# Reordering a four-layer network on one core: layer 0's attention as one chain, layer 2's attention behind the gathers row by row

## The chip, the cores and the metric

The kernel runs on one core of one Trainium2 chip. A core has a matrix engine (TensorE, "PE"; its weight loads are listed apart as "PEld"), a vector engine (VectorE, "DVE"), a scalar engine for activations (ScalarE, "ACT"), a general engine (GpSimd, "POOL") that also issues the indirect DMAs here, and a sync engine (SyncE, "SP") that issues most of the other DMAs. Each engine works through its own list of instructions in order and waits on semaphores of the others. The metric is the device time of one execution in microseconds. A profile is one execution taken by the hardware profiler; its span covers the first to the last recorded instruction.

## The reference

The input x has 4 rows of 1024 tokens with 128 features, in f32. Four layers follow, each an attention (or a recurrence) and a feed-forward, each added to x and normalised:

```
x = layernorm(x + L0_attn(x));  x = layernorm(x + L0_ffn(x))
x = layernorm(x + L1_attn(x));  x = layernorm(x + L1_ffn(x))
x = layernorm(x + L2_attn(x));  x = layernorm(x + L2_ffn(x))
x = layernorm(x + L3_attn(x));  x = layernorm(x + L3_ffn(x))
```

- L0_attn: a projection, a causal convolution over 4 tokens, and cumulative sums along the tokens: with v a projected value and p_w a positive weight, the sums of p_w·poly(v)·cos(theta·v), p_w·poly(v)·sin(theta·v) and p_w for 4 values of theta. The ratio, normalised by its mean square, goes through small matrices, a gate and an output projection.
- L0_ffn: x and the weight are rounded to a 6-bit float grid in blocks of 32 with a scale each, then one linear map.
- L1_attn: a diagonal complex recurrence, h[t] = a·h[t-1] + B·x[t], y = C·Re(h).
- L1_ffn: a mixture of 16 experts (4 chosen per token, within 2 of 4 groups) and a shared one; each is silu(x·gate)·(x·up)·down.
- L2_attn: causal softmax attention with 16 heads of 8 and rotary positions.
- L2_ffn: a mixture of 8 experts, 2 chosen, that share common matrices, each with a low-rank correction of rank 16.
- L3_attn: a gated mixing along the tokens with Toeplitz matrices. L3_ffn: 32 experts, 4 chosen, and a shared one.

A token's result in L0_attn and L1_attn depends on the earlier tokens of its row; in L2_attn it depends on all earlier tokens of the same row, in L3_attn on all tokens of its row. Rows are independent of each other, and the feed-forwards work token by token.

## The kernel before

**Tiles and parts.** x stays in SBUF as 32 tiles of 128 tokens. A "quarter" q is 256 tokens of each of the 4 rows, 8 tiles; quarters 0 and 1 are called the first half (part a), 2 and 3 the second half (part r in layer 1). Tile `q*8 + b*2 + k` holds the k-th 128 tokens of quarter q of row b.

**Mixtures of experts.** `l1_route` computes each token's experts and the place of each (token, expert) pair in a list sorted by expert. `spread` (L1305 on) then issues one indirect DMA per tile and chosen expert on POOL, 64 for a half in layer 1, each writing 128 rows of x to the list in HBM. `l1_experts` reads the list in blocks of 4 tiles (`xg`), transposes them, multiplies them with the weights of the block's expert (in a "wall" of all experts' weights in SBUF, 3 MB for layer 1) and writes the results to another list. `l1_close` gathers them back (`collect`, L1359: 64 indirect reads on POOL into buffers `yt`, four to a buffer, five buffers), adds them to x with the routing weights, normalises, saves x to HBM and makes the transposed xT that the next layer reads. `zero_lists` clears the lists first.

**The order of the work.** Each stage is a Python generator that emits instructions and yields a cost. `run` goes through one generator alone. `mix(main, side, pace, drain)` goes through `main` and, after each of its yields, takes from `side` until the yields' costs balance; what `side` emits is put on each engine's list behind the latest instruction of `main`. `chain` puts generators one behind the other, `abreast` lets several advance together by cost, `when` holds a generator back until a name is in `self.listed`, and `press` (L1824) draws from a side generator until a condition holds. A framework then orders each engine's list and puts in semaphores. The order of all stages is written out in `all()`:

1. `l0_attn` of quarters 0 and 1 alone. Its multiplications by `pq` go to POOL; with `no_pool` they go to DVE. `prepare(q+1)` is emitted within quarter q. For each of 4 thetas: t, k (the rounding of t, by adding and taking away a large number RND), sin and cos on ACT, a multiplication by pq, a scan on DVE (`l0_scan`), a square on ACT, matmuls.
2. `l1_setup`, `l2_setup`, then `l0_ffn` of quarters 0 and 1 alone (its `quantize` passes between DVE and POOL), then `l1_attn` of quarters 0 and 1 mixed with `l2_weights`. The latter builds the 24 weight tiles of layer 2's 8 experts: a small matrix `am` on POOL, matmuls, a copy on ACT, a write to HBM.
3. `l1_route(a)`. Then `l0_attn` of quarters 2 and 3 (no_pool) mixed with `spread` of part a.
4. `l1_wall` (weights), `l1_experts(a)` mixed with `l0_ffn` and `l1_attn` of quarters 2 and 3; `l1_shared(a)` and what is left of that, mixed with `l1_close(a)` quarter by quarter.
5. `l1_wall` again, `l2_attn(0)`, that is the first half's attention, mixed with `l1_route(r)` and `spread` of part r.
6. `l2_wall`, `l1_experts(r)` and `l1_shared(r)` mixed with layer 2's routing and spread of part a2; `l2_experts(a2)` mixed with `l1_close(r)`.
7. `l2_attn(1)` and all later stages.

`norm(tiles, by)` takes mean and variance on DVE, the reciprocal root on ACT, POOL or DVE by the argument `by`, and applies both with one DVE instruction a tile (L205).

## Time and profile before

| | us |
|---|---|
| median of 15 runs | 2542.91 |
| lowest, highest | 2538.28, 2558.33 |
| profiled execution, its own time | 2538.07 |
| its span | 2536.3 |

| stage (profiled execution) | about, us from the span's start |
|---|---|
| layer 0 attention, quarters 0 and 1 | 0 to 130 |
| layer 0 feed-forward, quarters 0 and 1 | 145 to 205 |
| layer 1 attention, quarters 0 and 1, with layer 2's weight tiles | 205 to 285 |
| layer 1 routing of part a | 285 to 312 |
| layer 0 attention, quarters 2 and 3, beside the spread of part a | 312 to 426 |
| layer 1 experts of part a | 434 to 540 |
| shared experts, rest of quarters 2 and 3 | 540 to 602 |
| gathers of part a | 541 to 648 |
| layer 2 attention, first half (first scores at 667.6) | to 928 |
| spread of part r, inside it | 726 to 807 |

How the profile is read: "busy" is the time in which an engine worked on instructions of a group or a stretch. A line of a group gives the source line, engine, operation, the tiles written and read, the count, the total and the mean duration of one, and behind the bar the idle time of the engine just before them and what ended it. A line of a stretch gives start and end, length, busy time and number of instructions for PE, PEld, DVE, ACT and POOL, the granted TensorE clock, the share of the DMA engines and GB/s. The chain of work is followed back from the last instruction: at each step to what released it, or to the instruction before it on its engine. "Another core or an unknown queue" and "remote" in it mean a wait whose end the profile cannot put down to a recorded instruction.

### The profile page before, as it was taken

Reading aid. Unit: us, or ns where it says so; the run is one execution under the profiler, and the core shown is the slowest. Engines: PE = TensorE matmul, PEld = TensorE weight load, DVE = VectorE, ACT = ScalarE, POOL = GpSimd, SP = SyncE. Lnnn points to the kernel's source line nnn. Section 1 sums busy time; section 2 is a strip of 40 time slices with the busy share of each in tenths; the row PEclk is TensorE's granted clock in tenths of the full one; section 3 lists DMA queues with packets and bytes.
Section 4 is the critical chain, followed back from the end, with each engine's and each line's share of the span. In section 5 each row is a group of like instructions: output and inputs, shape, how many; then the busy total and the mean of one; then the engine's idle time right before and its main releaser. Section 6 shows DMA issues by size and latency. Waiting matters only on the chain.

```text
span 2536.3 us, 28615 instructions
## 1 busy us (share of the span) xinstructions
PE 1698.1 (67%) x9605; PEld 1030.5 (41%) x9605; DVE 1350.1 (53%) x3797; ACT 810.8 (32%) x1158; POOL 779.7 (31%) x725
## 2 busy tenths in 40 slices
PE   7538676863652875797797888758619896754810
PEld 3225333752220454555432332336316683642710
DVE  8864796856560662344556663735403565631453
ACT  5512362320320432222375545512102352310310
POOL 5432185235145004233310001020560203154364
PEclk9768787986775997898898988979859997876965
DMA  9902002331001143222300000030410331321421
GB/s 318 289 16 83 19 35 105 104 129 42 21 28 40 53 147 107 73 62 61 110 20 1 1 6 12 14 128 22 176 57 18 106 105 44 92 85 53 117 77 53
DMA packets 224007, 192.05 MB, mean 76 GB/s; under 512 B 16816, under 2 KB 204080, under 8 KB 222832
## 3 DMA queue, kind: packets, MB, share of 16 engines
q1 hardware_dynamic: 203152, 147.28, 18.5%
q0 software_dynamic: 20704, 42.86, 5.1%
q8 instruction: 83, 1.36, 0.2%
q14 instruction: 68, 0.56, 0.1%
HBM read 93.47 MB, written 96.60 MB: 75 GB/s over the span
## 4 chain that ended last, share of the span: by engine, by line
PE 43%; DVE 22%; another core or an unknown queue 13%; POOL 9%; issue 8%; ACT 3%; DMA 3%; SPq 0%; DVEq 0%; POOLq 0%; ACTq 0%
PE gu L157 11%; PE s L157 10%; PE yp L157 5%; PE tp L165 5%; PE sc L157 5%; POOL l1ra L1293 4%; POOL yt L1293 2%; PE pu L157 2%; PE pg L157 1%; DVE x L1359 1%; PE py L157 1%; DVE pr L1055 1%; ACT pr L1049 1%; DVE x L205 1%
## 5 line engine op out<-in xcount | busy, mean ns | idle before, releaser
L1049 ACT ACTIVATE pr<-sc 128x1024 f32<-128x1024 f32 x288 | 279.5, 1021 | 319.2 <-PE sc L157 191.0
L157 PE MATMUL gu<-ld,xgT 128*128 x768 | 203.7, 408 | 47.4 <-DVE hg L1689 15.6
L157 PE MATMUL sc<-qm,kT 32*128 32x512 f32 (+3 forms) x1536 | 201.3, 559 | 15.6 <-ACT pr L1049 11.7
L157 PE MATMUL s<-pr,va 128*32 128x512 f32 (+3 forms) x1536 | 176.9, 526 | 48.2 <-issue 28.1
L157 PE MATMUL gu<-wall,xgT 128*128 x352 | 180.7, 640 | 20.1 <-DMA wall<-wall 18.0
L165 PE MATMUL tp<-ld,hg 128*128 128x128 f32 x736 | 118.8, 284 | 95.4 <-DVE hT L169 52.5
L157 PEld LDWEIGHTS gu<-ld,xgT 128*128 128x128 f32 x768 | 145.7, 201 | 79.4 <-issue 23.7
L169 DVE COPY hT<-tp 128x512 f32<-128x512 f32 x140 | 96.0, 686 | 138.5 <-remote 72.3
L165 PEld LDWEIGHTS tp<-ld,hg 128*128 128x128 f32 x736 | 94.5, 147 | 153.2 <-issue 58.9
L1055 DVE TENSOR_TENSOR pr<-pr,ld 128x512 f32<-128x512 f32 (+1 forms) x160 | 92.4, 580 | 102.2 <-ACT pr L1049 95.9
L1689 DVE TENSOR_TENSOR hg<-sg,gu 128x256 f32<-128x256 f32 x192 | 78.5, 417 | 123.6 <-ACT sg L1688 109.1
L1462 ACT ACTIVATE sg<-gu 128x512 f32<-128x512 f32 x88 | 52.5, 598 | 276.4 <-PE gu L157 166.8
L157 PEld LDWEIGHTS sc<-qm,kT 32*128 32x128 f32 x1536 | 86.3, 198 | 120.1 <-issue 73.7
L167 ACT COPY xgT<-tp 128x512 f32<-128x512 f32 x118 | 69.2, 586 | 182.0 <-PE tp L165 129.3
L1688 ACT ACTIVATE sg<-gu 128x256 f32<-128x256 f32 x192 | 72.9, 385 | 162.7 <-PE gu L157 105.0
L165 PE MATMUL tp<-ld,xg 128*128 128x128 f32 x472 | 78.9, 292 | 64.2 <-DMA xg<-l3rb 15.0
L1464 DVE TENSOR_TENSOR hg<-sg,gu 128x512 f32<-128x512 f32 x88 | 60.1, 683 | 112.4 <-ACT sg L1462 93.3
L1293 POOL DMA_INDIRECT l1ra<-x,posl1a x64 | 94.3, 1474 | 60.7 <-DVE posl1a L1270 41.5
L1293 POOL DMA_INDIRECT yt<-l1yr,posl1r x64 | 60.5, 945 | 151.4 <-DVE x L1359 82.0
L157 PE MATMUL yp<-ld,hT 128*128 x768 | 104.2, 278 | 4.3 <-issue 3.5
L157 PEld LDWEIGHTS s<-pr,va 128*32 128x32 f32 x1536 | 38.2, 111 | 157.9 <-issue 110.5
L157 PE MATMUL yp<-wall,hT 128*128 x704 | 99.9, 289 | 1.5 <-DVE hT L169 1.5
(433 smaller groups left out, 3529.5 us busy)
## 6 DMA issues: line engine op xcount, KB each, us to landing
wall<-wall SPq DMA_DIRECT2D x16, 768.0 KB
l3ra<-zero SPq DMA_DIRECT2D x1, 6144.0 KB
wall<-we SPq DMA_DIRECT2D x24, 256.0 KB
ld<-in_l_w SPq DMA_DIRECT2D x2, 3072.0 KB
ld<-in_l_w SPq DMA_DIRECT2D x1, 6144.0 KB
xg<-l3ra SPq DMA_DIRECT2D x24, 256.0 KB
l3ya<-yg SPq DMA_DIRECT2D x24, 256.0 KB
l1ra<-zero SPq DMA_DIRECT2D x1, 5120.0 KB
```

The lines of the kernel that those rows point to most:

```text
L157: return self.nc.tensor.matmul(out, lhsT, rhs, start=start, stop=stop)
L165: nc.tensor.transpose(pt[:, k * P : (k + 1) * P], s, self.ident)
L167: nc.scalar.copy(dst, pt[:, : n * P])
L169: nc.vector.tensor_copy(dst, pt[:, : n * P])
L205: nc.vector.tensor_scalar(x, x, mv[:, t, 0:1], rstd[:, t : t + 1], ALU.subtract, ALU.mult)
L1049: nc.scalar.activation(pr, sc[h], AF.Exp)
L1055: nc.vector.tensor_tensor(d, d, cst["tril"].unsqueeze(1).unsqueeze(1).to_broadcast([P, 2, n, P]), ALU.mult)
L1293: ins = self.nc.gpsimd.indirect_dma_start(**kw)
L1462: nc.scalar.activation(sg, gu[:, 0, :], AF.Silu)
L1464: nc.vector.tensor_tensor(h, sg, gu[:, 1, :], ALU.mult)
L1688: nc.scalar.activation(sg, pg[:, :, 0, :], AF.Silu)
L1689: nc.vector.tensor_tensor(h[:, 2 * c : 2 * c + 2, :], sg, pg[:, :, 1, :], ALU.mult)
```

## The change

- `l0_attn` takes all four quarters as one main generator; only quarter 3 has `no_pool`. Its side, at pace 0.8, is, in this order: layer 1's and layer 2's setup and the clearing of lists (`after(0)`), `l0_ffn` and `l1_attn` of quarter 0, the same of quarter 1, `l1_route` of part a1, and `spread` of a1 abreast of `l2_weights`. Part a1 is the first half with its tiles in the order of rows.
- `l1_shared(a1)` comes ahead of `l1_experts(a1)`; both are mixed with `l0_ffn` and `l1_attn` of quarters 2 and 3.
- `l1_close` goes by rows instead of quarters: 16 gathers, the additions, the norm of 4 tiles, the transposes, and the name "row" is listed. It now lies, with `l1_route(r)` and the spread of r, beside `l2_attn(0)`, whose `prepare(b)` presses the side until row b is listed.
- `l1_wall` for part r is loaded after `l2_attn(0)`, together with `l2_wall`.
- The first addition of the rounding (k) moves from DVE to ACT; the cosine is written over k; t, sq and den, and pools of `l0_ffn` and `l1_attn`, have fewer buffers.
- In layer 0 and in layer 1's attention the norm is applied on ACT (`on_act`), with a small extra DVE instruction; `am` moves from POOL to ACT; one multiplication of `l1_attn` in the first half moves from POOL to DVE.

```diff
+    def norm(self, tiles, by="act", on_act=False):
...
+        if on_act:
+            off = self.tile(self.small, [P, n], f"off{n}")
+            nc.vector.scalar_tensor_tensor(off, mv[:, :, 0], -1.0, rstd, ALU.mult, ALU.mult)
         for t, x in enumerate(tiles):
-            nc.vector.tensor_scalar(x, x, mv[:, t, 0:1], rstd[:, t : t + 1], ALU.subtract, ALU.mult)
+            if on_act:
+                nc.scalar.activation(x, x, AF.Identity, bias=off[:, t : t + 1], scale=rstd[:, t : t + 1])
+            else:
+                nc.vector.tensor_scalar(x, x, mv[:, t, 0:1], rstd[:, t : t + 1], ALU.subtract, ALU.mult)
...
-                    t = self.tile(tp, [P, QC], "t")
-                    nc.scalar.activation(t, xv, AF.Copy, scale=self.turn[:, m : m + 1])
+                    turn = self.turn[:, m : m + 1]
+                    t = self.tile(tp, [P, QC], "t", bufs=1)
+                    nc.scalar.activation(t, xv, AF.Copy, scale=turn)
                     k = self.tile(tp, [P, QC], "k")
-                    ts(k, t, RND, None, ALU.add)
+                    nc.scalar.activation(k, xv, AF.Identity, scale=turn, bias=self.rnd)
...
-                    re = self.tile(tp, [P, QC], "re")
+                    re = k
...
-                        times(v, v, pq, ALU.mult)
+                        times(q)(v, v, pq, ALU.mult)
...
+        nc, x, hf = self.nc, self.x, part.q0 // 2
+        xTv = self.xT.rearrange("p (q b t) -> p b q t", q=NQT, b=B)
+        for b in range(B):
+            yield from self.collect("l1", part, K1, yp, b * 4, 4)
+            tiles = part.order[b * 4 : b * 4 + 4]
+            self.norm([x[:, t, :] for t in tiles], by="dve")
+            for t in tiles[::2]:
+                nc.sync.dma_start(out=self.xsave[:, t : t + 2, :], in_=x[:, t : t + 2, :])
+            yield (5.0,)
...
+            nc.vector.tensor_copy(xTv[:, b, 2 * hf : 2 * hf + 2, :], pt.rearrange("p (q t) -> p q t", q=2))
+            self.listed.add(f"row {hf}{b}")
...
             def prepare(b):
+                self.press(side, lambda: f"row {hf}{b}" in self.listed)
...
-                    nc.gpsimd.tensor_scalar(am, ab[:, i, :], self.cst["em"][:, e : e + 1], 2.0, ALU.mult, ALU.mult)
+                    nc.scalar.activation(am, ab[:, i, :], AF.Copy, scale=em[:, e : e + 1])
...
+    def after(self, q):
+        yield from self.when(lambda: f"l0 {q}" in self.listed)
+        if q == 0:
+            self.l1_setup()
+            yield (20.0,)
+            self.l2_setup()
+            self.zero_lists("l1")
+            yield (4.0,)
...
-                self.run(self.l0_attn((0, 1)))
-                self.l1_setup()
-                self.l2_setup()
-                weights = self.l2_weights()
-                next(weights)
-                self.zero_lists("l1")
-                self.run(self.l0_ffn((0, 1)))
-                self.run(self.mix(self.l1_attn((0, 1)), weights))
-                self.run(self.l1_route(a))
-                self.run(self.mix(self.l0_attn((2, 3), True), self.spread("l1", a, K1)))
+                main = self.l0_attn(range(NQT), (NQT - 1,))
+                side = self.chain(
+                    *(g for q in range(2) for g in (self.after(q), self.l0_ffn((q,)), self.l1_attn((q,)))),
+                    self.l1_route(a1), self.abreast(self.spread("l1", a1, K1), self.l2_weights()),
+                )
+                self.run(self.mix(main, side, pace=0.8))
...
-                    side = self.chain(self.l0_ffn((2, 3), True), self.l1_attn((2, 3), True))
-                    self.run(self.mix(self.l1_experts(a, wall), side, drain=False))
-                    self.run(self.mix(self.chain(self.l1_shared(a), side), self.l1_close(a, yp)))
+                    side = self.chain(*(g for q in (2, 3) for g in (self.l0_ffn((q,)), self.l1_attn((q,)))))
+                    self.run(self.mix(self.chain(self.l1_shared(a1), self.l1_experts(a1, wall)), side))
+            with ExitStack() as c2:
+                yp = self.pool(c2, "l1ya", 5, right=True)
+                side = self.chain(self.l1_close(a1, yp), self.l1_route(r), self.spread("l1", r, K1))
+                self.run(self.mix(self.l2_attn(0, side), side))
             with ExitStack() as c2:
                 wall = self.l1_wall(c2)
-                self.run(self.mix(self.l2_attn(0), self.chain(self.l1_route(r), self.spread("l1", r, K1))))
                 wall2 = self.l2_wall(c2)
```

## The prediction

> **What bounds the kernel now.** I read the page first. No engine is full: TensorE is busy 67% of the span, and 13% of the chain that ended last is put down to nothing that the profile knows.
>
> ```profile
> PE 1698.1 (67%) x9605; PEld 1030.5 (41%) x9605; DVE 1350.1 (53%) x3797; ACT 810.8 (32%) x1158; POOL 779.7 (31%) x725
> PE 43%; DVE 22%; another core or an unknown queue 13%; POOL 9%; issue 8%; ACT 3%; DMA 3%; SPq 0%; DVEq 0%; POOLq 0%; ACTq 0%
> ```
>
> The built programs have the same order on every engine from the second layer 2 attention on (about 1250 us), so only the time before that can change. I cut it into stages; each line gives the stretch, its length and busy time per engine.
>
> ```profile
> 20.00:78.00 58.00, 45.52 (x171) 19.25 (x170) 52.47 (x42) 39.13 (x45) 34.75 (x12) 0.89 1.05 307
> 78.00:130.00 52.00, 29.80 (x129) 13.39 (x128) 42.06 (x53) 25.74 (x33) 19.78 (x8) 0.72 1.03 289
> 130.00:205.00 75.00, 25.75 (x123) 17.32 (x121) 46.92 (x123) 8.53 (x16) 22.92 (x15) 0.68 0.01 2
> 205.00:285.00 80.00, 66.48 (x269) 41.07 (x268) 36.14 (x90) 17.89 (x32) 16.51 (x23) 0.87 0.22 79
> 285.00:312.00 27.00, 21.14 (x68) 9.62 (x72) 22.69 (x124) 14.72 (x15) 0.00 (x0) 0.82 0.00 1
> 312.00:414.00 102.00, 74.24 (x332) 33.04 (x322) 94.00 (x120) 59.40 (x67) 85.47 (x55) 0.85 0.09 35
> ...
> 434.00:540.00 106.00, 92.57 (x580) 79.13 (x579) 84.27 (x212) 38.37 (x79) 18.96 (x8) 0.97 0.32 95
> 540.00:602.00 62.00, 35.00 (x140) 22.82 (x140) 30.41 (x76) 5.85 (x10) 34.41 (x32) 0.75 0.30 104
> 602.00:668.00 66.00, 17.77 (x57) 8.61 (x60) 37.59 (x154) 8.17 (x12) 31.70 (x33) 0.56 0.16 49
> 735.00:815.00 80.00, 16.61 (x68) 5.48 (x68) 7.54 (x33) 2.05 (x2) 54.98 (x58) 0.54 0.12 48
> ```
>
> The third number after a stretch's length is VectorE. It is slack in 130 to 285 (layer 0's feed-forward and layer 1's attention of the first half) and full in 312 to 414 (layer 0's attention of the second half beside the spread). In 735 to 815 nothing works but GpSimd, which issues the spread of the second half's rows, in the middle of layer 2's attention. The chain and the waits show that stall, and a smaller one at 554:
>
> ```profile
> 554.42 14.65 another core or an unknown queue
> ```
> ```profile
> 732.60 12.33 another core or an unknown queue
> 747.47 21.29 another core or an unknown queue
> 769.81 46.67 another core or an unknown queue
> ```
> ```profile
> ACT pr L1049 <- remote: 79.2, 2, 66.9
> ```
>
> The two spreads differ in one thing: VectorE was busy 0.92 beside the first, 0.09 beside the second.
>
> ```profile
> L1293 POOL DMA_INDIRECT l1ra<-x,posl1a x64 | 94.3, 1474 | 60.7 <-DVE posl1a L1270 41.5 <-issue 19.2
> L1293 POOL DMA_INDIRECT l1rr<-x,posl1r x64 | 61.8, 965 | 97.8 <-DVE posl1r L1270 78.6 <-issue 19.2
> ```
>
> With the 0.30 us of issue the slow one has a pitch of about 1.78, the fast one 1.27 us. Pairing each TensorE result in the trace with its first reader: the reader starts 0.06 us (mean of 1311) after TensorE's last record if GpSimd issued no indirect DMA in the 15 us before, 0.88 after 1 to 8, 2.13 after 9 to 11, and 7.47 (40 cases) after 12 or more. What makes that lag the trace does not say. I call it the crawl and use it as a price: a full-pitch burst nearly stops work that passes from TensorE to another engine.
>
> **Part by part**, against the profiled execution's 2538.07 us (median of the runs 2542.91, 4.8 above; I add the difference to the median).
>
> 1. Layer 0's attention in one chain, first half's next layers behind it. The first quarter has nothing beside it and ends at about 78, as before. VectorE's instructions up to the end of layer 1's routing, taken in the changed order at before's mean durations, are 282 us, 56 of them by 78. Cross-check: 316 to the experts' start before, less 16 rounding adds of 0.777 (now on ScalarE), 19 of normalisations (ScalarE too), 9 multiplies of 1.215 (third quarter, now GpSimd), plus about 4 for the additions, is 277 with a 4 us tail behind routing: 273. ScalarE gains this work and has room: the same count gives it 184. At 0.92, the row of 312 to 414, the remaining 226 take 246: routing ends at 324 (before 312). Ends: 304 at a full VectorE, 354 at the 0.81 of 78 to 130.
>
> 2. The spread begins there, but only a 4 us tail of layer 0's attention is left for VectorE, so it runs at 1.27: 81 us, to 405 (before 426). What stood beside the old spread stood 102 us; now little is beside it. GpSimd's queue holds layer 0's feed-forward of the third quarter behind the spread.
>
> 3. Layer 2's weight tiles moved from beside layer 1's attention (where they cost nothing visible) to beside the spread. On TensorE's queue all 24, then the shared experts and that feed-forward, stand ahead of the experts. A tile passes TensorE to ScalarE with two PSUM buffers: at the crawl (7.5 + 0.6 copy + 1.2 back) / 2 = 4.65 us, so from 331 (half of the layer 1 wall's 9 us of DMA behind routing) 16 are done at 405; 8 at 1.83 (44 us of TensorE in 24) end at 420. Then shared experts 23 (38 before less the 14.65 stall) and 6 for the feed-forward's interleaved matmuls (its GpSimd chain, 16 us from 444 to 460 before, runs 409 to 425 alongside). Experts start at 450, before 434: +16. Ends: 415 without any crawl; 493 if TensorE makes 0.6 records per us, half of the old stall's 104 in 81 us: the 72 tile and 8 attention matmuls then end at 464, plus 29. On SP the experts' wall waits behind twelve of the tiles' writes and for layer 0's last matmuls, so it is late with them, not besides.
>
> 4. Experts and the rest of the side. By the count of part 1 VectorE has 111 us to do between the end of layer 0's attention and that of layer 1's attention of the fourth quarter, some 16 of them before the experts; the 95 left, the 0.795 of 434 to 540, are 119: 569, before 602. The gain so far is 33.
>
> 5. Closing by rows. Two rows' 32 gathers, between 1.25 and the 1.67 of this stage: 45, then 20 from the last gather to the first scores as before (648 to 667.6): 634, before 667.6. **Gain 33.** The title's "first row" is two in VectorE's order: rows 0 and 1 both stand ahead of the attention's main work.
>
> 6. The other two rows' gathers now lie inside layer 2's attention. Twenty may run ahead (five buffers of four) and come at full pitch: 25 us at 75 lost of 81 is 23. The other twelve 3. VectorE gets 22 us of adds and norms there, of which its idle 0.27 takes most: 7. **+33**; ends 0 (gathers thinned out, below 9 in 15 us) and 50. ScalarE and TensorE queue behind VectorE's block of 44 instructions.
>
>    The Trainium skill ("SBUF — State Buffer", "A bandwidth-pool intuition that's wrong") says that a DMA with descriptors made by GpSimd took about 620 ns alone and 3100 beside VectorE's copies. Here the row beside a VectorE at 0.92 is 1474 against 965 ns. No row comes near 3100. By the page's figure 32 gathers would be 99 us instead of 45, an estimate, and the sum some 50 us higher.
>
> 7. The second spread moves from 35% to 82% of layer 2's attention, with 128 TensorE instructions left; the old stall let 104 through in 81 us. So it costs the same there, plus its last landing now open (431 less 426 before): **+4**. Ends -10 and +25.
>
> 8. Layer 1's wall, 3 MB, was loaded at 541 under other work; now it waits for the end of layer 2's first attention, behind five expert loads on SP and ahead of layer 2's wall. Its first load took from 420 to about 430: **+10**. Ends 0 (under the spread) and 20.
>
> 9. Normalisation on ScalarE elsewhere, 16 saves for 4, ScalarE instead of GpSimd for small scalings: off the path while the spreads and VectorE bound; nothing. Without that cover, 16 issues on SP at the 0.3 of a GpSimd issue are 5 us.
>
> Sum: -33 + 33 + 4 + 10 = **+14**. 2543 + 14 = **2557 us**.
>
> **Rivals.**
> - *Faster (0.32).* The weight tiles and rows do not crawl. With parts 1 and 3 at 415, experts and side end at 534, first scores at 599 (-69); of part 6 the 7 remain, the rest as above: -69 + 21 = -48; halfway -20. For it: the lag was seen mostly with attention's two passes per tile, and the old first spread had none. Against: that spread was slow. It decides from experts earlier than 436.
> - *Much slower (0.17).* The exposed spread crawls at 0.6 records per us, experts at 493: +57. For it: the 735 to 815 line. Against: copies to ScalarE need one pass only.
> - *Wash (0.09).* As my case, but the gathers inside the attention take 20 instead of 33: +1.
> - *Not what it says (0.08).* If the attention in effect waits for all four rows, gathers of 107 us as before from 569 give scores at 696: the gain of 33 becomes 28 lost, but part 6 vanishes: +42.
>
> **Numbers.** My case, +5 to +35 (2548 to 2578), has 0.34, little more than the faster one, from which the crawl alone parts it; I take it because the row nearest to the new first spread is the second of before, at full pitch with VectorE idle. With the two slower rivals, slower has 0.59. A measurement of this kernel tells about 0.2%, 5 us, from no change: within it lies the wash, 0.09; faster has 0.32. The range leaves a tenth out at each end: below, the faster case's better third (from -40, 2503, to -48 and past it); above, what goes beyond the much slower case's +57 with a few microseconds of parts 7 and 8 (2607).
>
> **What would show it.** Right: first spread's indirects near 0.97 us and VectorE idle beside it, weight tiles unfinished at its end, experts around 450, first scores around 634, a stall of about 80 us late in the first layer 2 attention, then a 10 us hole before the experts of the second half. Wrong: routing after 350 (VectorE starved by one-buffer tiles of layer 0), experts before 436, scores before 610, or a difference that arises after 1250.

## The result

The changed kernel takes 2657.78 us (median of 9 runs, 2645.94 to 2665.94); before took 2543.2 (47 runs). The ratio is 1.0444, 95% interval 1.0429 to 1.0459: 4.4% slower, 115 us, where 14 us slower was forecast and the range ended at 2607. The profiled execution took 2647.2 us, 109.1 more than the one of before; the sums below are made on that pair.

The page of the changed kernel: first line busy time, second the chain that ended last.

```profile
PE 1733.5 (66%) x9605; PEld 1038.8 (39%) x9605; DVE 1340.0 (51%) x3872; ACT 857.9 (32%) x1270; POOL 765.5 (29%) x709
PE 43%; DVE 20%; issue 13%; another core or an unknown queue 13%; POOL 4%; ACT 3%; DMA 3%; SPq 0%; DVEq 0%; POOLq 0%; ACTq 0%
```

VectorE and GpSimd have a little less to do than before (1340.0 for 1350.1 us, 765.5 for 779.7). ScalarE has 47 us more, which the change moved there, and TensorE's same 9605 instructions take 35 us more, at a mean granted clock of 0.810 instead of 0.825. That is less than half of the 109 us on either engine, and both are idle for longer than before; what grew most is waiting, and with it the chain's "issue" (8% before, 13% now). The stages show where (stretch, length, busy time of PE, PEld, DVE, ACT, POOL, granted TensorE clock, DMA share, GB/s):

```profile
20.00:110.00 90.00, 67.73 (x243) 29.89 (x241) 55.21 (x42) 60.71 (x69) 37.89 (x14) 0.89 1.06 294
110.00:380.00 270.00, 172.26 (x694) 85.07 (x694) 216.40 (x529) 130.34 (x181) 79.45 (x30) 0.77 0.07 18
...
380.00:461.00 81.00, 26.64 (x60) 11.99 (x58) 7.00 (x14) 8.07 (x19) 61.52 (x64) 0.58 0.26 99
461.00:502.00 41.00, 30.27 (x103) 16.57 (x104) 3.98 (x20) 16.14 (x37) 0.00 (x0) 0.84 0.47 180
...
893.00:973.00 80.00, 20.13 (x96) 8.00 (x96) 9.34 (x35) 3.98 (x4) 60.79 (x64) 0.56 0.13 52
```

The stretch from 110 to 380 is layer 0's chain with the first half's next layers beside it. VectorE, which was to be full there, is busy 216.4 of 270, or 0.80. From 380 to 461 the first spread runs with almost nothing beside it, and TensorE still needs 41 us for the rest of the weight tiles. From 893 to 973 the other engines nearly stand still beside the second spread, as before, only later. The spreads themselves (group lines: count, total busy, mean ns of one, idle time before) have the forecast duration now that VectorE is idle beside both:

```profile
L1309 POOL DMA_INDIRECT l1ra<-x,posl1a x64 | 61.8, 966 | 39.0 <-DVE posl1a L1286 19.8 <-issue 18.3 <-DMA l1ra<-x,posl1a 0.6
L1309 POOL DMA_INDIRECT l1rr<-x,posl1r x64 | 61.3, 958 | 140.1 <-issue 140.1
```

In the chain of waits of the changed kernel (start, us, what), the holes lie in and behind the bursts of indirect DMAs: two of the weight tiles' waits, the gathers of the first two rows, the two in the second spread, and at the end the load of layer 1's wall.

```profile
407.95 12.49 issue
...
442.34 23.62 issue
...
656.48 39.95 another core or an unknown queue
...
905.17 29.16 another core or an unknown queue
935.71 47.03 another core or an unknown queue
...
1003.15 10.95 DMA ld<-in_l_w
```

The first instructions of each stage in the traces, in us. An exponential is an instruction of the attention's softmax on ScalarE; for the last one the time is its end. The last two columns are from other chips, of which the experiments tell; "before" there is b_thin, which has the time of before within 0.1%.

| event | before | changed | before, other chip | changed, other chip |
|---|---|---|---|---|
| first spread, first and last DMA | 312, 425 | 380, 460 | 319, 429 | 381, 461 |
| weight tiles, start of the last copy | 258 | 502 | 259 | 450 |
| first half's experts, first matmul | 436 | 537 | 437 | 488 |
| layer 2 attention, first and last exponential | 667, 911 | 716, 995 | 652, 820 | 642, 840 |
| second spread, first DMA | 726 | 893 | 711 | 816 |
| second half's experts, first matmul | 919 | 1014 | 828 | 918 |
| layer 2's first spread | 948 | 1043 | 857 | 947 |
| layer 2's first row gathers | 1240 | 1353 | 1075 | 1164 |
| span | 2536 | 2645 | 2161 | 2257 |

### The profile page after: what moved, and what is told of

The parts are those of the page before. It is cut to its first block, busy times and chain, and to the rows that moved or that the text cites. A ratio compares the mean times of both kernels' runs of the same rounds, so it can differ in the third digit from the quotient of the medians.

```text
span 2645.3 us, 28805 instructions
## 1 busy us (share of the span) xinstructions
PE 1733.5 (66%) x9605; PEld 1038.8 (39%) x9605; DVE 1340.0 (51%) x3872; ACT 857.9 (32%) x1270; POOL 765.5 (29%) x709
## 4 chain that ended last, share of the span: by engine, by line
PE 43%; DVE 20%; issue 13%; another core or an unknown queue 13%; POOL 4%; ACT 3%; DMA 3%; SPq 0%; DVEq 0%; POOLq 0%; ACTq 0%
PE gu L159 11%; PE s L159 10%; PE sc L159 5%; PE yp L159 5%; PE tp L167 4%; PE pu L159 2%; DVE x L1375 1%; PE pg L159 1%; DVE s L367 1%; PE py L159 1%; PE z L159 1%; POOL l3rb L1309 1%; PE s L167 1%; DVE pr L1071 1%
## 5 line engine op out<-in xcount | busy, mean ns | idle before, releaser
L1309 POOL DMA_INDIRECT l1rr<-x,posl1r x64 | 61.3, 958 | 140.1 <-issue 140.1
```

The source lines that it names most:

```text
L1309: ins = self.nc.gpsimd.indirect_dma_start(**kw)
```

## The experiments

The runs fell on several chips, and the kernel before does not take the same time on all of them: 2543 us on the first chip and on that of the second group below, 2164 to 2168 on all others. Every comparison is therefore with before on the same chip; a result is given as its median, its ratio to before and, in brackets, the 95% interval of the ratio. Apart from the numbered parts of the prediction, "part one" below is the change up to the first half's experts (layer 0 in one chain with the next layers, the spread and the weight tiles beside it), "part two" the closing by rows beside layer 2's attention, with the second spread behind it and the wall loaded after it.

What differs is the stall in the bursts of indirect DMAs. ScalarE has the same 1158 instructions in before (first chip) and in b_thin (first group). Set side by side, the former lag by less than 2 us up to 541 us, by 17 more after the gathers of part a, by 75 more after the second spread, and by 377 in all at the end; after 541 us the lag grows by 12 to 80 in most bursts, and by less than 5 in any stretch between them. The mean granted clock is 0.825 against 0.873, but away from the bursts the two run alike: from 434 to 540 us, where no indirect DMA is issued, it is 0.97 and 0.96, and TensorE's 580 instructions take 92.6 and 93.0 us. I call chips "with" and "without the stall".

### First group, without the stall (before 2164.4 us)

**a_chain_undone**: the changed kernel with part one undone.

```diff
...
-                main = self.l0_attn(range(NQT), (NQT - 1,))
...
-                self.run(self.mix(main, side, pace=0.8))
+                self.run(self.l0_attn((0, 1), ()))
+                self.l1_setup()
...
+                self.run(self.mix(self.l1_attn((0, 1)), weights))
+                self.run(self.l1_route(a1))
+                self.run(self.mix(self.l0_attn((2, 3), (2, 3)), self.spread("l1", a1, K1)))
...
-                    self.run(self.mix(self.chain(self.l1_shared(a1), self.l1_experts(a1, wall)), side))
+                    self.run(self.mix(self.l1_experts(a1, wall), side, drain=False))
+                    self.run(self.mix(self.l1_shared(a1), side))
```

> The changed kernel with part one undone: layer 0's attention, feed-forward, layer 1's attention, routing, spread and weight tiles in the order of before, the experts before the shared ones; part two (closing by rows inside layer 2's attention, wall loaded after it) stays. Theory: part two alone costs what the trace of after shows from the first scores to the second half's experts, 300 us against 247, less some 10 won before the first scores: 2583 us (2560 to 2600). Rival, all of the loss sits in part one: 2543 within 10. Rival, part two costs most and part one little: 2640 or more.

Measured: 2266.6 us, ratio 1.0469 (1.0451 to 1.0486), 102 slower. The absolute figures of the expectation were for the wrong chip; by ratio the 2583 would be 1.016. Here the experts start at 466, 29 later than before, the attention's first exponential comes at 658 (before 652), its last at 854 (820), and then the second spread, which began at 829, runs on to 909 with nothing beside it: the second half's experts start at 929 instead of 828. So what this kernel loses on this chip is above all the late spread.

**a_rows_undone**: part two undone; all rows are closed before the attention, with nothing beside them.

```diff
+                    yp = self.pool(c2, "l1ya", 5, right=True)
+                    self.run(self.l1_close(a1, yp))
             with ExitStack() as c2:
-                yp = self.pool(c2, "l1ya", 5, right=True)
-                side = self.chain(self.l1_close(a1, yp), self.l1_route(r), self.spread("l1", r, K1))
-                self.run(self.mix(self.l2_attn(0, side), side))
-            with ExitStack() as c2:
                 wall = self.l1_wall(c2)
+                side = self.chain(self.l1_route(r), self.spread("l1", r, K1))
+                self.run(self.mix(self.l2_attn(0, side), side))
```

> The changed kernel with part two undone: all four rows are closed before layer 2's attention starts, the wall is loaded before it, routing and spread of the second half stand beside it from its start as before; part one stays. Theory: 53 us won back inside the attention, 35 to 50 lost to gathers with nothing beside them: 2640 us (2625 to 2660). Rival, part one does not cost anything by itself and the loss is part two's: 2560 or less.

Measured: 2222.4 us, 1.0259 (1.0229 to 1.0289), 58 slower. Without part two the kernel is slower too, and neither theory's number can be read off another chip. The experts start at 487, 50 later than before (437), the gathers at 589 instead of 543, and the first exponential comes at 693, 40 later: most of the loss is there by then. The attention takes 175 us with the spread inside it; before took 167.

**a_weights_early**: the weight tiles beside layer 1's attention of quarter 1 (`within` draws two tiles after each of its yields).

```diff
-                    *(g for q in range(2) for g in (self.after(q), self.l0_ffn((q,)), self.l1_attn((q,)))),
-                    self.l1_route(a1), self.abreast(self.spread("l1", a1, K1), self.l2_weights()),
+                    self.after(0), self.l0_ffn((0,)), self.l1_attn((0,)),
+                    self.after(1), self.l0_ffn((1,)), self.within(weights, self.l1_attn((1,))),
+                    self.l1_route(a1), self.spread("l1", a1, K1),
```

> The changed kernel with layer 2's weight tiles moved from beside the spread to beside layer 1's attention of quarter 1. Theory: the shared experts then start at the spread's end or earlier instead of 41 us after it; the experts at about 495 instead of 536, the time 2618 us (2605 to 2635), less if routing gets later by the tiles. Rival, the spread holds up whatever stands there and the shared experts wait as long: 2650 to 2665.

Measured: 2296.9 us, 1.0601 (1.0584 to 1.0619); the whole change has 1.0393 on such a chip (a_third), so this is 44 us worse. The tiles push the end of routing from 381 to 427. They are not free in front of routing. The expectation was for a chip with the stall, where this did not run.

**b_thin**: the kernel before with a GpSimd instruction behind each indirect DMA of the second spread.

```diff
                 done.append(ins)
+                if lay + part.name == "l1r":
+                    nc = self.nc
+                    nc.gpsimd.tensor_scalar(self.fill, self.fill, 1.0, None, ALU.mult)
```

> The kernel before, with one GpSimd multiplication of a 128x128 tile (about 0.46 us, result unused) behind each indirect DMA of the second spread, so that its pitch is about 1.75 us as in the first spread. Theory, the stall comes from the pitch of the indirect DMAs: it goes, the spread ends at about 840 beside running attention, 40 to 55 us won: 2495 us (2485 to 2515). Rival, the first spread was harmless because VectorE was busy or each DMA holds the others up for the same time whatever the pitch: 2540 to 2580.

Measured: 2165.9 us, 1.0007 (0.9998 to 1.0017). Inconclusive as it was meant: the multiplications had no tie to the DMAs and moved ahead of the first spread (271 to 318 us; it starts at 319 here, at 312 in b_thin2 below); the second spread's pitch is 1.33. But the trace tells the main thing. This is the second spread's stretch:

```profile
711.00:795.00 84.00, 68.87 (x595) 32.84 (x587) 59.87 (x156) 36.84 (x38) 64.79 (x64) 0.91 0.23 89
```

Beside the same 64 DMAs TensorE makes 595 instructions, where on the first chip it made 68 in 80 us. So the stall does not belong to the program alone.

### Second group, with the stall (before 2544.3 us)

**a_again**: the changed kernel, no edit.

> The changed kernel as it is, on the chip of these runs. The kernel before took 2164 us on the chip of the first experiments and 2543 on the first chip; there the trace shows no stall during the second half's spread (TensorE made 605 records in it, not 104). Theory: on a chip without the stall the change costs nearly the same, because the spread of the second half, hidden in the attention before, is now left over behind it: about +100, 2266 us (2245 to 2290) against 2164. Rival, the two parts' losses of 102 and 58 us add up: 2320 or more. Rival, the loss on the first chip was the stall's: within 20 of before.

Measured: 2646.5 us, 1.0408 (1.0373 to 1.0444). This chip has the stall, so the expectation's question was not put; the first result is repeated.

**a_route_early**: routing abreast of the closing.

```diff
-                side = self.chain(self.l1_close(a1, yp), self.l1_route(r), self.spread("l1", r, K1))
+                side = self.chain(self.abreast(self.l1_close(a1, yp), self.l1_route(r)), self.spread("l1", r, K1))
```

> The changed kernel with the routing of the second half emitted abreast of the closing by rows instead of behind it, so that the second spread starts right behind the last gathers (about 760 us) and not at 830 to 890. Theory: on a chip without the stall it hides in the attention again, 50 to 60 us won against the changed kernel on the same chip; on one with the stall, less than 15. Rival, GpSimd is not what the second half's experts wait for, the wall and the attention's end are: within 10 on both.

Measured: 2655.3 us, 1.0456 (1.0415 to 1.0496): no gain. The spread now stands at 790 to 870, well inside the attention (734 to 1007), and the attention is as long as with the spread at its end (273 us, a_again 274). In this pair the place of the spread did not matter where there is the stall, as part 7 of the prediction had it.

**a_bufs**: layer 0's buffers given back.

```diff
-                den = self.tile(bp, [P, QC], "den", bufs=1)
+                den = self.tile(bp, [P, QC], "den")
...
-                    t = self.tile(tp, [P, QC], "t", bufs=1)
+                    t = self.tile(tp, [P, QC], "t")
...
-                    re = k
+                    re = self.tile(tp, [P, QC], "re", bufs=1)
...
-                        sq = self.tile(tp, [P, QC], "sq", bufs=1)
+                        sq = self.tile(tp, [P, QC], "sq")
```

> The changed kernel with layer 0's buffers given back as far as they fit: den, t and sq double again, the cosine in a tile of its own (single). Theory A, the single tiles make the engines wait for each other and keep VectorE at 0.82 instead of 0.92: routing ends 20 us or more earlier (380 to 360 or less), and so does the kernel. Theory B, it is the order, VectorE's queue in which two chains of passes wait for GpSimd and ScalarE in turn: within 5 us.

**a_nopool**: the products of quarters 1 and 2 on VectorE.

```diff
-                main = self.l0_attn(range(NQT), (NQT - 1,))
+                main = self.l0_attn(range(NQT), (1, 2, 3))
```

> The changed kernel with the multiplications by pq of quarters 1 and 2 on VectorE instead of GpSimd (18 of 1.22 us more for VectorE, 18 of 2.4 to 4.3 less for GpSimd). Theory: VectorE's waits for these products (16 us listed between 78 and 380) and the GpSimd queue between the two chains go, routing ends 10 to 20 us earlier in spite of the 22 us of work. Rival, VectorE's work is the bound there: routing 15 to 22 later.

Measured: a_bufs 2648.4 us, 1.0411 (1.0377 to 1.0446), routing at 380 as without it; a_nopool 2628.2 us, 1.0348 (1.0303 to 1.0392), routing at 362 instead of 381. The stretch up to routing, a_bufs:

```profile
110.00:380.00 270.00, 161.72 (x649) 82.22 (x647) 215.03 (x510) 124.85 (x175) 71.16 (x28) 0.75 0.06 18
```

and a_nopool:

```profile
110.00:362.00 252.00, 157.14 (x658) 79.85 (x656) 213.93 (x521) 130.19 (x182) 26.90 (x13) 0.79 0.07 19
```

The single buffers that a_bufs gave back (layer 0's attention) are not what holds routing up: with them doubled the first quarter's additions come 5 to 9 us earlier (100 and 105 instead of 109 and 110), VectorE works 67.6 instead of 55.4 us from 20 to 110, and routing still ends at 380. Those of `l0_ffn` and `l1_attn` were not tried. Moving 18 products to VectorE, more work for the engine that was taken as the bound, brought routing 20 us forward and the end 18: its share of this stretch rises from 0.80 to 0.85, GpSimd's busy time there falls from 79 to 27. So VectorE was in part waiting, not working, and GpSimd's products were a part of what held it up.

### Third group, without the stall (before 2166.1 us)

**b_thin2**: as b_thin, the multiplications held in place.

```diff
+                    behind = mybir.DependencyInfo(mybir.DependencyClass.NoSync, mybir.DependencyReason.DATA)
+                    if last:
+                        self.tc.add_manual_dep(ins.ins, last.ins.name, behind, reason="queued behind")
+                    last = self.nc.gpsimd.tensor_scalar(self.fill, self.fill, 1.0, None, ALU.mult)
+                    self.tc.add_manual_dep(last.ins, ins.ins.name, behind, reason="queued behind")
```

> The kernel before, with one GpSimd multiplication of a 128x128 tile (about 0.46 us, result unused) held in place between every two indirect DMAs of the second spread (in the earlier try the multiplications had moved away from them). Pitch about 1.75 us, VectorE as idle as before. On a chip with the stall (before at about 2543 us): theory, the pitch makes it, the spread takes 112 us and the attention goes on beside it, 2500 us or less. Rival, each indirect DMA holds the others up whatever the pitch, or VectorE's being busy protected the first spread: 2560 to 2580. On a chip without it (2164): within 10 us of before.

It ran twice more, on two other chips (b_thin2_again, b_thin2_third), and they had no stall either.

> The kernel before with a GpSimd multiplication held between every two indirect DMAs of the second spread, once more, for a chip with the stall; so far it ran on one without (before at 2166 us: 12 us slower, pitch 1.80, TensorE 7.0 records per us as without it). On a chip with the stall (before at about 2543): theory, the pitch makes the stall: 2500 us or less and TensorE at 3 records per us or more in the spread. Rival, the indirect DMAs hold the others up whatever the pitch: 2555 to 2585, TensorE below 1.5. On a chip without it: 12 us slower again.

> The kernel before with a GpSimd multiplication held between every two indirect DMAs of the second spread, once more; both runs so far were on chips without the stall (12 us slower). On a chip with it: theory, the pitch makes the stall, 2500 us or less; rival, the DMAs hold the others up whatever the pitch, 2555 to 2585.

Measured: 2178.1, 2179.0 and 2181.1 us; 1.0069, 1.0062 and 1.0071 (intervals within 1.0043 to 1.0092). The second spread of b_thin2_again:

```profile
709.00:830.00 121.00, 92.73 (x847) 46.22 (x847) 82.44 (x219) 50.40 (x52) 107.80 (x127) 0.92 0.16 62
```

At a mean pitch of 1.9 (median 1.8) TensorE makes 7.0 instructions per us, as at 1.33 (595 in 84). Without the stall the pitch makes no difference to TensorE's pace, and the longer spread costs 11 to 17 us. Whether a wider pitch would avoid the stall where there is one stays open.

**a_weights_late**: the tiles beside the first half's experts.

```diff
-                    self.l1_route(a1), self.abreast(self.spread("l1", a1, K1), self.l2_weights()),
+                    self.l1_route(a1), self.spread("l1", a1, K1),
...
-                    side = self.chain(*(g for q in (2, 3) for g in (self.l0_ffn((q,)), self.l1_attn((q,)))))
+                    side = self.within(self.l2_weights(), self.chain(*(g for q in (2, 3) for g in (self.l0_ffn((q,)), self.l1_attn((q,))))))
```

> The changed kernel with layer 2's weight tiles moved from beside the first spread to beside the experts of the first half. Theory: on a chip with the stall the experts start at about 490 instead of 537, as only the shared experts and the feed-forward stand in front of them; the 44 us of TensorE come back beside the experts, some 35 of them on the path: 10 to 20 us won, 2630 us against 2647. Rival, the tiles hide beside the experts: 40 to 50 won. On a chip without the stall: within 20 of the changed kernel.

Measured: 2312.8 us, 1.0687 (1.0664 to 1.071), 60 us more than the whole change on such a chip, where at most 20 were expected; what it does with the stall was not measured. The stages of experts and of what is left:

```profile
486.00:590.00 104.00, 95.94 (x574) 78.98 (x574) 64.46 (x161) 47.31 (x107) 9.47 (x4) 0.98 0.38 115
590.00:655.00 65.00, 47.50 (x174) 27.19 (x174) 27.33 (x96) 22.81 (x50) 3.25 (x4) 0.83 0.23 77
```

TensorE is full beside the experts (95.9 of 104), so the rest of the tiles stands behind them, and the gathers start at 651 instead of 590. The experts begin at 486, and with the tiles in front of them at 488: without the stall the tiles hide under the spread.

**a_close_r**: the second half closed by quarters as before.

```diff
-        self.both = (Part("a", 0, 2, range(B)), Part("r", 2, 2, range(B)))
+        self.both = (Part("a", 0, 2, range(B)), Part("r", 2, 2))
...
-                side = self.l1_close(r, yp)
+                side = self.l1_close_q(r, yp)
```

> The changed kernel with the second half closed quarter by quarter as before (part r in the order of quarters); the first half stays by rows. Theory: the 14 to 19 us by which the changed kernel falls back further after the second half's experts (its distance to before is 95 us at layer 2's first spread and 109 at the end) come from closing r by rows; they come back, 2632 us against 2647 on a chip with the stall. Rival, they come from the walls or from the longer gathers whatever the order: within 5 us.

Measured: 2244.0 us, 1.0363 (1.0338 to 1.0388). The interval overlaps that of the whole change on such a chip (1.0362 to 1.0424, a_third); with the stall it did not run. From layer 2's first spread to its first row gathers it takes 213 us, the change (a_third) 217, b_thin 218: a few microseconds where there is no stall. With it, before takes 292 there and the change 310; where these 18 come from was not shown.

**b_act**: of the change only ScalarE's part in layer 0's quarters 2 and 3, in the kernel before.

```diff
-                    ts(k, t, RND, None, ALU.add)
+                    if no_pool:
+                        nc.scalar.activation(k, xv, AF.Identity, scale=self.turn[:, m : m + 1], bias=self.rnd)
+                    else:
+                        ts(k, t, RND, None, ALU.add)
...
-                self.norm(self.quarter(q), by="act" if no_pool else "pool")
+                self.norm(self.quarter(q), by="act" if no_pool else "pool", on_act=no_pool)
```

> The kernel before, with the first rounding addition and the norm of quarters 2 and 3 of layer 0's attention on ScalarE as in the change (8 additions of 0.7 and 16 norm instructions of 0.38 us less for VectorE), nothing else. Theory, VectorE bounds 312 to 414: 8 to 12 us faster. Rival, ScalarE's longer chain or the spread beside it takes its place: within 4 us of before.

Measured: 2161.5 us, 0.9979 (0.9962 to 0.9995): 4.6 us faster, 1 to 8 by the interval, so between theory and rival. It is the only kernel here that is faster than before, on a chip without the stall; with it, it did not run.

### The last runs, without the stall

**a_chain_undone_again** and **a_third** (before 2167.6 us):

> The changed kernel with part one undone, once more, for a chip with the stall (on one without it was 102 us slower than before). On a chip with the stall: theory, the late second spread is no dearer than the stalled one of before, part two costs 34 inside the attention, 11 behind it and 18 at the closing of r, less a few won in front: 2590 us (2575 to 2610). Rival, part two costs its 102 there too: 2645.

> The changed kernel as it is. On a chip without the stall (before at about 2165 us) it has not run; from its parts there (experts of the first half 50 us later than before, attention 25 longer, the second spread 60 us behind it instead of inside) theory says 90 us slower, 2255 (2245 to 2270). Rival, the parts' 58 and 102 add: 2320. On a chip with the stall: 2647 to 2658 again.

Measured: a_chain_undone_again 2270.5 us, 1.0474 (1.0444 to 1.0503), as on the first of these chips; how the parts divide the loss where there is the stall was not measured. a_third 2253.2 us, 1.0393 (1.0362 to 1.0424), 86 slower, as the theory said (2255). So the change costs much the same with the stall (1.0408 and 1.0444) and without (1.0393). The losses of the two parts (102 with part one undone, 58 with part two undone) do not add: without the stall the whole change loses less than its second part alone. There its first exponential even comes 10 us earlier than before (642, 652); the attention is then 30 us longer and the second half's experts start 90 us later (918, 828). The same stretches of a_third, spread, experts' start, experts, second spread and what follows it:

```profile
381.00:462.00 81.00, 61.69 (x217) 33.93 (x217) 16.00 (x43) 29.06 (x63) 61.78 (x64) 0.85 0.52 195
462.00:488.00 26.00, 16.65 (x78) 11.74 (x77) 16.67 (x28) 3.79 (x7) 9.61 (x5) 0.87 0.11 34
488.00:588.00 100.00, 89.01 (x564) 76.72 (x563) 75.89 (x195) 44.57 (x101) 9.48 (x4) 0.97 0.37 105
...
816.00:897.00 81.00, 23.85 (x225) 12.73 (x225) 23.60 (x72) 11.63 (x12) 61.79 (x64) 0.66 0.13 52
897.00:918.00 21.00, 8.19 (x33) 7.00 (x34) 7.08 (x31) 2.45 (x3) 0.56 (x1) 0.58 0.65 225
```

All 24 tiles' copies start by 450 here; on the first chip 8 of 24 start before the spread's end. What ScalarE's copy waits for, first the changed kernel on the first chip, from 390 to 505 (total us, times, longest):

```profile
ACT we L1427 <- issue: 61.7, 8, 23.6
```

("issue" is a wait for nothing that the profile shows), then a_third:

```profile
ACT we L1427 <- PE s L159: 14.5, 13, 2.1
```

From 816 to 897 there is simply little left to do: of TensorE's 225 instructions, 193 come by 840, where the attention ends; then it waits for the spread and behind it for the wall.

**b_rows** (before 2164.6 us): b_act and closing by rows, with the spread and the wall early.

```diff
             with ExitStack() as c2:
                 wall = self.l1_wall(c2)
-                self.run(self.mix(self.l2_attn(0), self.chain(self.l1_route(r), self.spread("l1", r, K1))))
+                with ExitStack() as c4:
+                    yp = self.pool(c4, "l1ya", 5, right=True)
+                    on = self.chain(self.abreast(self.l1_close_rows(a1, yp), self.l1_route(r)), self.spread("l1", r, K1))
+                    self.run(self.mix(self.l2_attn(0, on), on))
```

> The kernel before with ScalarE's share of b_act, and of the change only this: part a in the order of rows, closed by rows beside the first half of layer 2's attention, which waits for its rows; but the wall is loaded before the attention as before, and the second half's routing is emitted abreast of the closing, so that the second spread starts behind the last gathers. Theory: what made part two dear without the stall (102 us) is the second spread and the wall left behind the attention; with both back inside it the closing by rows costs within 20 us of before (2145 to 2190 against 2166; with the stall 2530 to 2575 against 2544). Rival, the gathers and adds inside the attention are dear by themselves: 40 us slower or more.

**a_route_wall** (before 2166.5 us): the changed kernel with both early.

```diff
+                wall = self.l1_wall(c2)
-                side = self.chain(self.l1_close(a1, yp), self.l1_route(r), self.spread("l1", r, K1))
+                side = self.chain(self.abreast(self.l1_close(a1, yp), self.l1_route(r)), self.spread("l1", r, K1))
...
             with ExitStack() as c2:
-                wall = self.l1_wall(c2)
```

> The changed kernel, whole, with the second half's routing emitted abreast of the closing by rows and the wall loaded before layer 2's first attention. Theory for a chip without the stall: the late second spread and the wall are most of the change's 86 us there (2253 against 2167); the second half's experts start right behind the attention, about 850 instead of 918, the whole near 2195 (2180 to 2215). Rival, the first half's experts, 50 us late, bound: 2230 or more. On a chip with the stall: 2640 to 2660, as the spread stalls the attention wherever it stands.

Measured: b_rows 2175.7 us, 1.0043 (1.003 to 1.0055), 11 slower than before and by ratio 14 slower than b_act; a_route_wall 2193.1 us, 1.0127 (1.011 to 1.0144), 27 slower where the whole change has 86. Both came out as their theories said. Without the stall, the late second spread and the late wall are some 59 us of the change's 86. Closing by rows beside the attention costs 14 us in the kernel before, where the quarters' closing stood beside other work; with layer 0 in one chain the runs point the other way: a_route_wall (1.0127) is 29 us faster than a_rows_undone (1.0259), whose gathers stand alone. These two differ also in the place of the second half's routing, and they ran on different chips.

## Why the prediction was wrong

It was right that the change is slower, and on most of the parts, and wrong by 95 us on the pair of profiled executions (101 on the medians), most of it in two terms.

- **Part 1, routing at 324: it is 380.** This is the step that failed, in both of its numbers. "The first quarter has nothing beside it and ends at about 78" was read into the profile: VectorE's 52 us from 20 to 78 were taken for the first quarter's, while a part of them was the second quarter's, made beside it. The additions to x that end the quarter start at 113 in before and at 110 in the changed kernel. That is 32 us later than 78, with 216 us of work left instead of 226, which is 11 less at 0.92: 21 us. "At 0.92, the row of 312 to 414" was the second: that row is a stage whose products all run on VectorE. In the new chain two of the three remaining quarters send them to GpSimd, and a second chain with GpSimd passes stands in the same queues; VectorE gets to 0.80, 216 in 270 instead of 235: 35 us. 21 + 35 is the 56. With the products on VectorE (a_nopool) routing comes 20 us earlier. What makes up the other 36 stays open: the order's other waits are the likely cause, but no run shows it, and it is not layer 0's single buffers (a_bufs). The prediction's own sign, "routing after 350", came true, but not with the cause that it gave in brackets, those one-buffer tiles. The work itself, 282 us, was right: 271.6 from 20 to 380 and 7.8 before. (The end of 354 given for a share of 0.81 is 357 by its own numbers.)
- **Part 2, pitch 1.27 and 81 us:** as forecast.
- **Part 3, experts 45 us after the spread's end: 76.** The mechanism, tiles that crawl beside the spread, was right on that chip and the price too low. A tile was put at 4.65 us, two overlapping; after the first five the copies came at 420, 431, 441 and 466, 10 to 25 us apart. Eight were done at the spread's end, not 16, and the sixteen left took 41 us instead of 15 for eight: 26 of the 31 us. On a chip without the stall the experts start 27 us after the spread (461 to 488).
- **Part 4, 119 us for experts and side:** 120 (537 to 657).
- **Part 5, 65 us more to the first scores:** 59 to the first exponential. The 40 us hole in the chain at 656 is in it.
- **Part 6, +33 inside the attention:** 278 us from first to last exponential instead of 244, +34. The size fits; that the gathers alone make it was not tested on a chip with the stall. The Trainium skill's figure for a DMA with descriptors made by GpSimd beside VectorE's copies ("SBUF — State Buffer", "A bandwidth-pool intuition that's wrong"), about 3100 ns, would have added some 50 us, as the prediction estimated; nothing like it shows, for the 64 gathers of part a take 995 ns on average (1033 before). Single DMAs do come near it: the longest of these gathers takes 2.9 us, and 8 of the 64 DMAs of the first spread of before, beside a busy VectorE, take 2.4 to 3.01 us.
- **Parts 7 and 8, +14:** from the last exponential to the second half's experts 19 instead of 8 us, +11, the wall's load 10.95 of it.
- **Part 9, nothing: +14.** The stretch from layer 2's first spread to its first row gathers, with the closing of r by rows beside layer 2's first experts, took 18 us longer (310 instead of 292). It lies before the 1250 us after which the order is the same, and no part of the sum had priced it; 4 us came back from there to the end.

In sum 14 + 56 + 31 + 1 - 6 + 1 - 3 + 14 = 108 of the 109 us. The rival "much slower" had one of the two places right (the exposed spread), with experts 88 us after the spread's end where 76 were measured; what its 57 lacks is nearly the 56 of part 1, which it kept. The faster rival's premise, that the tiles do not crawl, holds on the chips without the stall; there the change is slower all the same, most of it for what parts 7 and 8 had priced at 4 and 10: with no stall, a spread and a wall left behind the attention are a loss of their own, some 59 of 86 us.

## What to carry to other kernels

A busy share is a row of a stage with its own mix of engines: before it is used for a stage that is put together anew, check by the end of a real step (here the additions to x at 113) which work the stretch's busy time belongs to, and whether the work that filled the engine comes along. Where two chains that pass between engines are merged into in-order queues, the engine that looks like the bound may be waiting, and a step moved onto it can win time, as a_nopool did. A long burst of DMA issues needs work beside it at its place in the order; count what is left there. On the chips with the stall that did not help (a_route_early).

## What the runs showed of the hardware

The same program takes 2543 us on the first chip and on the second group's, and 2164 to 2168 on the others. In the stretch that was compared, nearly all TensorE and VectorE work stops on the former while GpSimd issues indirect DMAs at the same pitch as on the latter (1.27 to 1.33 us). The DMA records of that stretch, the kernel before on the first chip from 735 to 815:

```profile
q0 software_dynamic: 1856, 3.80, 12.0%
q14 instruction: 1, 0.01, 0.0%
```

and b_thin from 711 to 795, without the stall:

```profile
q0 software_dynamic: 2015, 4.13, 12.6%
q1 hardware_dynamic: 288, 3.28, 9.7%
q8 instruction: 4, 0.07, 0.4%
```

The indirect DMAs move the same data at the same share. On the first chip no block of instructions comes through q8 in those 80 us, on the other four do. In the records the missing blocks do not look like the cause: the chain's three holes there end at 745, 769 and 816.5 us, while no q8 block comes between 722 and 818, so none of them ends with one (a single q14 block comes at 772, inside the third). What ends the holes the records do not tell. The first spread of before, at a pitch of 1.8 with VectorE busy, shows no such stall on the first chip: three q8 blocks come in it, as on the other chip, and ScalarE's lag behind b_thin grows by 0.4 us. What spares it, the pitch or the other work, is open as well.
